# Attention scores from two float32r parts, two heads in the two halves of the array's rows

## The chip, the core and the metric

The kernel runs on one core of a Trainium2 chip. The core has a matrix engine (PE, with its weight loads shown apart as PEld), a vector engine (DVE), a scalar engine (ACT), a general engine (POOL) and SP, which here only issues DMAs. Each engine works through its own instructions in order and waits on semaphores. PE writes to PSUM, eight banks of 128 partitions by 2 KB; DVE and ACT read PSUM, POOL and the DMAs do not. The metric is device time in microseconds. Before the change it was 4454.7 us (median of three runs, 4446.5 to 4455.5).

## The reference

Four attention blocks in a row act on `x` of 16 batches, 512 tokens and 256 channels, all float32, with 16 heads of 16 dims. Each is `x = x + block(layernorm(x))`:

```python
x = x + _L0_attn_a_ref(_layernorm(x), ...)   # causal mask, biases
x = x + _L0_ffn_ref(_layernorm(x), ...)      # tokens in two groups by a similarity, 5 register tokens
x = x + _L0_attn_b_ref(_layernorm(x), ...)   # rotary embedding, no mask
x = x + _L0_ffn_ref(_layernorm(x), ...)
```

Each block projects Q, K and V, takes softmax(Q K^T / 4) over 512 keys, multiplies by V and projects back. In block `f` a token attends only to the tokens of its own group (similarity to a given direction, scaled over the whole batch, above 0.9 or not) and to the registers; the register tokens get the mean of both groups' answers. The similarity of all batches must be known before the first scores of `f`.

## The kernel before, in words

The layers are called 0 (`a`), 1 (`f`), 2 (`b`) and 3 (`f`); `PLAN` lists them. A layer goes through 16 batches, a batch through four *quads* of four heads (`quads`), a quad through four key tiles of 128 (`t`).

**Two sets of scores.** Each head's scores are computed twice. `maxima` (L523) computes them with queries on the partitions, `s` (L545), and DVE takes each row's maximum (L547; in layer 0 with the causal mask added, L552). `finish` and `put` split the maxima into two bf16 numbers, turn them on PE (`mt`, L579), copy them on ACT (`ms`, L581), write them to DRAM (`md`, L583) and from there into two rows of the Q stack (L585). `products` (L594) computes the scores again with keys on the partitions, `t` (L612); those two rows subtract each query's maximum inside the matmul. In layer 0 another matmul adds the causal mask (L620). ACT takes the exponential (`e`, L623), and `weigh` multiplies by V in float32, four heads side by side in four 32-column tiles of the array (`po`, L634).

**Precision.** Q and K are split into three bf16 parts (`split3`, L329) and written to DRAM (`qd`, `kd`). `load_half` (L489) gathers six blocks of 16 rows for eight heads: 96 rows whose product sums the six largest part products. Rows 96 and 97 carry the group flags (from `fd`), 98 and 99 the maxima. There are three such stacks of Q and of K (`NB`), loaded by SP's DMAs.

**Other work** is cut into pieces by generators: `prep` (layer norm, projections, splits, similarity) for the next layer's batch, `tail` (division by the sums, output projection) of the batch before, `registers`, `masked`. `drain` deals pieces out between the scores by the costs that they yield. They use PSUM through `small` (pool `ps_s`, two banks); the scores use `ps_x`, five banks.

**Order.** The last loop (L919) issues four products per key tile, and `advance` runs `maxima` ahead by `AHEAD` = 36 heads' tiles; a quad's `put` follows `WAIT` = 8 steps after its last maximum. A list scheduler then fixes the order of instructions on each engine when the kernel is built. Before the first `f` scores all similarities must be in (`split`), so work does not run ahead across that point.

Of the kernel before, what the change touches and what calls it, by code (L numbers as in the profile page):

```python
# [39 lines left out]
H, D = 16, 16  # L41
# [6 lines left out]
RW = 4 * (32 + REG)  # L48
# [6 lines left out]
AHEAD = 36  # L55
WAIT = 8
QPARTS = (0, 1, 2, 0, 1, 0)
KPARTS = (0, 0, 0, 1, 1, 2)
ROWS = 96
# [3 lines left out]
def constants():  # L63
# [7 lines left out]
    c["mask_t"] = np.ascontiguousarray(f(-BIG) * up.T)  # L71
# [4 lines left out]
    c["cos"], c["sin"] = np.repeat(cos, H, axis=0), np.repeat(sin, H, axis=0)  # L76
    c["hm"] = np.concatenate([np.tile(np.eye(H, dtype=f), (8, 1)), np.zeros((P, H), f)], axis=1)
    blk, half = np.zeros((P, H, HV), f), np.zeros((P, REG), f)
    rows = np.zeros((2, 2, RW), f)
    for h in range(H):  # L80
        p, k = 32 * (h // 4), h % 4
        for r in range(REG):
            blk[p + REG * k + r, h] = 1.0
            half[p + REG * k + r, r] = 0.5
            rows[1, :, (32 + REG) * k + r] = 1.0
    c["blk"], c["half"], c["rows"] = blk, half, rows
    clamp = np.full((P, NT, 4), -MASKED, f)
    clamp[P - 1, NT - 1] = 3.0e38
    c["clamp"] = clamp
    reg = np.zeros((P, B, NT), f)  # L90
# [7 lines left out]
def hybrid_kernel(ctx: ExitStack, tc: tile.TileContext, a: dict, out: bass.AP):  # L98
# [3 lines left out]
    def pool(name, bufs, **kw):  # L102
# [10 lines left out]
        pool("pe", 9),  # L113
# [5 lines left out]
    ps_x = pool("ps_x", 5, space=PSUM)  # L119
    ps_o = pool("ps_o", 1, space=PSUM)  # L120
    ps_s = pool("ps_s", 2, space=PSUM)
# [17 lines left out]
    qd = [dram.tile([3, C, S], BF, tag=f"qd{b}", name=f"qd{b}") for b in range(B)]  # L139
    kd = [dram.tile([3, C, S], BF, tag=f"kd{b}", name=f"kd{b}") for b in range(B)]  # L140
    vd = [dram.tile([P, NT, VW], F32, tag=f"vd{b}", name=f"vd{b}") for b in range(B)]
    xd = [dram.tile([P, NT, C], F32, tag=f"xd{b}", name=f"xd{b}") for b in range(B)]
    fd = dram.tile([4, B, S], BF, tag="fd", name="fd")
    md = [dram.tile([NT, 2, 4, P], BF, tag=f"md{i}", name=f"md{i}") for i in range(8)]
# [10 lines left out]
    ident_bf = const.tile([P, P], BF, tag="ident_bf", name="ident_bf")  # L155
    nc.vector.tensor_copy(ident_bf, ident)
# [5 lines left out]
    def load_weights(layer, project):  # L162
# [7 lines left out]
        for i in ws:  # L170
            raw = ptmp.tile([P, 2, C], F32, tag="tmp", name=f"wraw{layer}_{i}")
            nc.sync.dma_start(raw, a[f"{kind}_w"][:, :, i, :])
            if i == WQ:
                nc.vector.tensor_scalar(raw, raw, SCALE, None, ALU.mult)
            k = 0 if project else i
            nc.scalar.copy(wh[:, :, k, :], raw)
            nc.vector.tensor_tensor(wl[:, :, k, :], raw, wh[:, :, k, :], ALU.subtract)
# [9 lines left out]
    bqk = load_const("bqk", [P, 2, 2])  # L187
# [6 lines left out]
    NB = 3  # L194
    Qs, Ks = [], []
    for i in range(NB):
        q = res.tile([P, 8, S], BF, tag=f"qs{i}", name=f"qs{i}")
        k = res.tile([P, 8, S], BF, tag=f"ks{i}", name=f"ks{i}")
# [8 lines left out]
    for i in range(2):  # L207
        t = res.tile([ROWS + 2, 2, RW], BF, tag=f"rst{i}", name=f"rst{i}")
# [3 lines left out]
    def constant_rows():  # L212
        both = ptmp.tile([4, 2, S], BF, tag="tmp", name="zo")
        nc.vector.memset(both[:, 0], 0.0)
        nc.vector.memset(both[:, 1], 1.0)
        for q, k in zip(Qs, Ks):
            for i, t in enumerate((q, k)):
                nc.sync.dma_start(t[ROWS : ROWS + 4], both[:, i].unsqueeze(1).to_broadcast([4, 8, S]))
        for t in rst:
            nc.gpsimd.memset(t, 0.0)  # L220
# [4 lines left out]
    def early_constants():  # L225
        late["mask_s"] = to_bf("mask_s", [P, S])
        late["mask_t"] = to_bf("mask_t", [P, P])
        late["clamp"] = load_const("clamp", [P, NT, 4])
# [4 lines left out]
    def direction():  # L233
# [13 lines left out]
        )  # L247
        ps = small("gt")
        for i in range(2):
            nc.tensor.transpose(ps[:, i * P : (i + 1) * P], g2[:, i * P : (i + 1) * P], ident)  # L250
# [5 lines left out]
    def late_constants():  # L256
# [7 lines left out]
        rows = p1.tile([2, 2, RW], F32, tag="rows", name="rows")  # L264
        nc.sync.dma_start(rows, a["rows"])
        rb = p1.tile([2, 2, RW], BF, tag="rb", name="rb")
        nc.vector.tensor_copy(rb, rows)
        for t in rst:
            nc.sync.dma_start(t[ROWS : ROWS + 2], rb)
# [5 lines left out]
    def prep(layer, b, x):  # L275
# [53 lines left out]
        def split3(which, i, y):  # L329

            t = p4.tile([P, 3, S], BF, tag="parts", name=f"t{which}{n}_{i}")
            nc.scalar.copy(t[:, 0, :], y)  # L332
            sub = nc.vector if which == "k" and layer + b == 0 else nc.gpsimd
            sub.tensor_tensor(y, y, t[:, 0, :], ALU.subtract)  # L334
            nc.vector.tensor_copy(t[:, 1, :], y)  # L335
            sub.tensor_tensor(t[:, 2, :], y, t[:, 1, :], ALU.subtract)  # L336
            d = (qd if which == "q" else kd)[b]
            nc.sync.dma_start(d[:, i * P : (i + 1) * P, :].rearrange("k p q -> p k q"), t)

        def parts(which, i):  # L340
            ps = small(f"p{which}{n}_{i}")
            yield from project(ps, WQ if which == "q" else WK, i)
            y = ptmp.tile([P, S], F32, tag="tmp", name=f"y{which}{n}_{i}")
            if kind == "a":
                w = 0 if which == "q" else 1
                nc.scalar.activation(y, ps, AF.Identity, bias=bqs[:, w, i : i + 1])
            else:
                nc.scalar.copy(y, ps)
            if kind == "f" and which == "q":
                y2 = ptmp.tile([P, S], F32, tag="tmp", name=f"y2{n}_{i}")  # L350
                nc.scalar.activation(y2, ps, AF.Square)
                st["y", i] = y, y2
            else:
                split3(which, i, y)

        def similar():
# [6 lines left out]
            for i in range(2):  # L363
                split3("q", i, st["y", i][0])
# [14 lines left out]
            else:  # L379
                nc.gpsimd.tensor_tensor(nd[:, 0], nd[:, 0], nhalf, ALU.pow)  # L380
# [4 lines left out]
        def turned(which):  # L385
# [10 lines left out]
            nc.vector.tensor_tensor(b_, y[1], sin, ALU.mult)  # L396
            nc.gpsimd.tensor_tensor(a_, a_, b_, ALU.subtract)
            nc.vector.tensor_tensor(b_, y[0], sin, ALU.mult)
            nc.gpsimd.tensor_tensor(y[1], y[1], cos, ALU.mult)
            nc.gpsimd.tensor_tensor(y[1], y[1], b_, ALU.add)  # L400
            split3(which, 0, a_)
            split3(which, 1, y[1])
# [47 lines left out]
    def split(layer):  # L450
# [22 lines left out]
        fl = p1.tile([P, 4, n], BF, tag="fl", name=f"fl{layer}")  # L473
# [4 lines left out]
        pf = small(f"pf{layer}", BF)  # L478
        for k in range(4):
            nc.tensor.transpose(pf[:n, k * P : (k + 1) * P], fl[:, k, :], ident_bf)  # L480
        fs = p1.tile([n, 4, P], BF, tag="fs", name=f"fs{layer}")
        nc.vector.tensor_copy(fs.rearrange("r k p -> r (k p)"), pf[:n, : 4 * P])
        nc.sync.dma_start(fd.rearrange("k b (t p) -> (b t) k p", p=P), fs)


    halves = [(layer, b, u) for layer in range(len(PLAN)) for b in range(B) for u in range(2)]
    cleared = set()

    def load_half(i):  # L489
        layer, b, u = halves[i]  # L490
        kind = PLAN[layer]
        q, k = Qs[i % NB], Ks[i % NB]
        hs = slice(8 * u, 8 * (u + 1))
        if kind == "b" and i % NB not in cleared:
            cleared.add(i % NB)
            nc.gpsimd.memset(q[ROWS : ROWS + 2].bitcast(F32), 0.0)
        for dst, src, blocks in ((q, qd[b], QPARTS), (k, kd[b], KPARTS)):
            src = src.rearrange("k (d h) s -> (k d) h s", h=H)
            r = 0
            while r < 6:  # L500
                e = r + 1
                while e < 6 and blocks[e] == blocks[e - 1] + 1:
                    e += 1
                p0 = D * blocks[r]
                nc.sync.dma_start(dst[D * r : D * e], src[p0 : p0 + D * (e - r), hs, :])
                r = e
        if kind == "f":
            f = slice(ROWS, ROWS + 2)
            nc.sync.dma_start(q[f], fd[0:2, b, :].unsqueeze(1).to_broadcast([2, 8, S]))
            nc.sync.dma_start(k[f], fd[2:4, b, :].unsqueeze(1).to_broadcast([2, 8, S]))  # L510
# [12 lines left out]
    def maxima(i):  # L523
# [490 lines left out]
```

## Time and profile before

| | |
|---|---|
| profiled execution | 4459.0 us, its span 4457.3 us |
| runs | 4446.5, 4454.7, 4455.5 us |
| granted PE clock, mean | 0.972 |
| busy: PE, DVE, ACT, POOL | 4232, 3392, 2791, 1483 us |
| layers 0, 1, 2, 3, from where their first scores stand | about 60, 1280, 2320, 3480 us |
| PE busy per 200 us in layers 0, 1, 2, 3 | 181 to 190, 199, 198, 193 to 195 |
| DVE busy per 200 us there | 132 to 147, 169 to 176, 153, 160 |
| DMA share in the same layers | 0.45 to 0.51, 0.44, 0.42, 0.40 |
| DMA traffic | 470.6 MB, 42.6% of 16 engines' span |

A group line names the source line, engine, operation, tiles written and read with their shapes, the number of instructions, their busy time and the mean ns of one, then the engine's idle time just before them and what ended most of it. Tile names: `s` and `t` are scores, `e` their exponentials, `po` the weighted sums, `md` the maxima in DRAM, `p..`, `x..`, `ot`, `pa`, `pj`, `r.` the work in between.

### The profile page before, as it was taken

Reading aid. Unit: us, or ns where it says so; the run is one execution under the profiler, and the core shown is the slowest. Engines: PE = TensorE matmul, PEld = TensorE weight load, DVE = VectorE, ACT = ScalarE, POOL = GpSimd, SP = SyncE. Lnnn points to the kernel's source line nnn. Section 1 sums busy time; section 2 is a strip of 40 time slices with the busy share of each in tenths; the row PEclk is TensorE's granted clock in tenths of the full one; section 3 lists DMA queues with packets and bytes.
Section 4 is the critical chain, followed back from the end, with each engine's and each line's share of the span. In section 5 each row is a group of like instructions: output and inputs, shape, how many; then the busy total and the mean of one; then the engine's idle time right before and its main releaser. Section 6 shows DMA issues by size and latency. Waiting matters only on the chain.

```text
span 4457.3 us, 76135 instructions
## 1 busy us (share of the span) xinstructions
PE 4231.9 (95%) x26672; PEld 1995.5 (45%) x26672; DVE 3392.3 (76%) x8003; ACT 2791.5 (63%) x5480; POOL 1482.9 (33%) x1302
## 2 busy tenths in 40 slices
PE   6999899999979999999999999999999799999999
PEld 4555555555534444444444444444444233333333
DVE  6776666777668888888888777777775687887885
ACT  3555455555536767767767666666666466666666
POOL 4445455554432433433433333423424100000000
PEclk8999999999979999999999999999999799999999
DMA  6544545454424444444444443444444144333441
GB/s 176 128 128 122 134 119 141 123 144 116 119 71 101 105 110 108 104 114 103 108 115 107 106 110 101 102 107 103 104 105 113 44 89 89 83 78 83 89 89 30
DMA packets 230020, 470.56 MB, mean 106 GB/s; under 512 B 45630, under 2 KB 176004, under 8 KB 205060
## 3 DMA queue, kind: packets, MB, share of 16 engines
q1 hardware_dynamic: 229636, 465.69, 42.6%
q8 instruction: 211, 3.46, 0.3%
q14 instruction: 173, 1.42, 0.1%
HBM read 291.18 MB, written 174.19 MB: 104 GB/s over the span
## 4 chain that ended last, share of the span: by engine, by line
PE 75%; DMA 12%; DVE 4%; ACT 3%; POOL 2%; issue 2%; SPq 1%; ACTq 0%; POOLq 0%; DVEq 0%
PE po L634 19%; PE t L612 17%; PE s L545 16%; DMA md<-ms 5%; PE pj L833 4%; PE pq L324 3%; PE pv L415 3%; PE pk L324 3%; ACT e L623 3%; DMA x<-in_x 2%; PE ot L793 2%; DMA qs<-qd 2%; PE rs L675 1%; DMA qs<-md 1%; DVE mx L547 1%
## 5 line engine op out<-in xcount | busy, mean ns | idle before, releaser
L623 ACT ACTIVATE e<-t 128x512 f32<-128x512 f32 (+1 forms) x3776 | 2053.4, 594 | 865.7 <-PE t L612 588.7
L547 DVE TENSOR_REDUCE mx<-s 128x1 f32<-128x512 f32 x3072 | 1970.6, 682 | 517.0 <-PE s L545 507.2
L612 PE MATMUL t<-qs,ks 100*128 100x512 bf16 (+3 forms) x4096 | 1422.6, 364 | 61.1 <-DMA qs<-md 37.5
L545 PE MATMUL s<-ks,qs 98*128 98x512 bf16 (+4 forms) x4096 | 1404.9, 367 | 57.9 <-DMA ks<-fd 16.9
L634 PE MATMUL po<-e,v 128*32 128x512 f32 (+1 forms) x8192 | 1071.1, 569 | 7.5 <-ACT e L623 4.9
L612 PEld LDWEIGHTS <-ks 100*128 100x128 bf16 x4096 | 397.8, 98 | 779.1 <-issue 528.9
L545 PEld LDWEIGHTS <-qs 96*128 96x128 bf16 (+1 forms) x4096 | 386.0, 99 | 597.9 <-issue 383.3
L552 DVE CUSTOM_DVE_ANT_0 sc<-s,mask_s_bf 128x128 bf16<-128x128 f32 (+3 forms) x1024 | 497.7, 486 | 172.5 <-PE s L545 134.6
L634 PEld LDWEIGHTS po<-e,v 128*32 128x32 f32 x8192 | 172.2, 108 | 407.6 <-issue 290.2
L380 POOL TENSOR_TENSOR nd<-nd,nhalf 128x64 f32<-128x64 f32 x30 | 316.8, 10561 | 0.0
L290 POOL TENSOR_SCALAR st<-mv 128x4 f32<-128x4 f32 x64 | 16.0, 251 | 884.3 <-DVE mv L287 849.7
L664 POOL COPY rst<-qs 96x40 bf16<-96x40 bf16 x64 | 14.6, 229 | 859.6 <-DMA qs<-qd 336.4
L334 POOL TENSOR_TENSOR yq<-yq,tq 128x512 f32<-128x512 f32 x112 | 131.1, 1177 | 296.9 <-ACT e L623 155.7
L650 ACT COPY o<-po 128x512 f32<-128x512 f32 x256 | 150.8, 589 | 110.5 <-PE po L634 107.8
L789 POOL TENSOR_TENSOR x<-x,f_bo 128x1024 f32<-128x1024 f32 x32 | 76.0, 2376 | 404.2 <-DMA x<-xd 308.1
L620 PE MATMUL t<-mask_t_bf,ident_bf 128*128 128x128 bf16 x1024 | 203.8, 223 | 0.0
L793 PE MATMUL ot<-ident,o 128*128 128x128 f32 x1024 | 182.7, 291 | 18.1 <-DVE vst L427 12.4
L306 POOL TENSOR_SCALAR xn<-x,nm,st 128x256 f32<-128x256 f32 x256 | 142.4, 561 | 116.0 <-PE xp L310 102.7
L332 ACT CAST tk<-yk 128x512 bf16<-128x512 f32 x112 | 69.3, 619 | 173.1 <-DMA qd<-tq 170.3
L793 PEld LDWEIGHTS ot<-ident,o 128*128 128x128 f32 x1024 | 129.4, 148 | 78.0 <-DVE vst L427 15.2
L336 POOL TENSOR_TENSOR tk<-yk,tk 128x512 bf16<-128x512 f32 x110 | 128.3, 1168 | 95.5 <-DVE tk L335 89.8
L335 DVE CAST tq<-yq 128x512 bf16<-128x512 f32 x112 | 88.6, 793 | 77.3 <-POOL yq L334 76.8
(365 smaller groups left out, 5509.4 us busy)
## 6 DMA issues: line engine op xcount, KB each, us to landing
ks<-kd SPq DMA_DIRECT2D x256, 256.0 KB
qd<-tq SPq DMA_DIRECT2D x128, 384.0 KB
qs<-qd SPq DMA_DIRECT2D x128, 384.0 KB
kd<-tk SPq DMA_DIRECT2D x128, 384.0 KB
vd<-vst SPq DMA_DIRECT2D x64, 576.0 KB
v<-vd SPq DMA_DIRECT2D x64, 576.0 KB
qs<-qd SPq DMA_DIRECT2D x128, 256.0 KB
ks<-kd SPq DMA_DIRECT2D x256, 128.0 KB
```

Of the source, the lines that this page charges most:

```text
L324: nc.tensor.matmul(dst, ww[:, c, w, cols], xx[:, c, :], start=(k == 0 and c == 0), stop=(k == 2 and c == 1))
L380: nc.gpsimd.tensor_tensor(nd[:, 0], nd[:, 0], nhalf, ALU.pow)
L545: nc.tensor.matmul(ps, q[rows, h, t * P : (t + 1) * P], k[rows, h, :end], start=True, stop=True)
L547: nc.vector.tensor_reduce(st["mx"][:, t, j : j + 1], ps, AX.X, ALU.max, negate=True)
L552: nc.vector.tensor_tensor_reduce(w, ps, late["mask_s"][:, S - end :], 1.0, -3.0e38, ALU.add, ALU.max, st["mx"][:, t, j - m + 1 + i : j - m ...
L612: nc.tensor.matmul(ps, k[: ROWS + 4, h, t * P : (t + 1) * P], q[: ROWS + 4, h, q0:], start=True, stop=(kind != "a"),)
L620: nc.tensor.matmul(ps[:, :P], ident_bf, late["mask_t"], start=False, stop=True)
L623: st["exp", t] = nc.scalar.activation(e[:, : m * w], st["ps"][:, : m * w], AF.Exp)
L634: mm = nc.tensor.matmul(st["po"][32 * j : 32 * j + 32, q0:], v[:, t, h * HV : h * HV + 32], E.pop((t, j)), start=(t == 0), stop=(t == NT - 1),
L650: nc.scalar.copy(o, st["po"])
L793: nc.tensor.transpose(ps[:, g * P : (g + 1) * P], O[layer, b, g][:, t * P : (t + 1) * P], ident)
L833: nc.tensor.matmul(ps[:, k * C : (k + 1) * C], aa[:, k, c, :], ww[:, c, 0, :], start=(q == 0 and c == 0), stop=(q == 2 and c == 1),)
```

## The change

Q and K are split into two float32r parts, and a head's stack has 48 rows (three blocks of 16) and four more for maxima and flags. Two heads of a pair take partitions 0 to 63 and 64 to 127. Each pair's two matmuls write two neighbouring PSUM banks, and one reduction and one exponential serve both. The stacks, with their constant rows and flags, stand in DRAM as the array reads them; a quad of Q or K comes by one GpSimd DMA. The maxima of eight heads go back together. `ps_x` has three tiles of two banks, `ps_s` one bank. Some rotary products move from DVE to POOL; the long power on POOL is cut into four.

```diff
-AHEAD = 36
-WAIT = 8
-ROWS = 96
+AHEAD = 24
+WAIT = 3
+ROWS = 48
+HALF = 64
...
-        pool("pe", 9),
+        pool("pe", 5),
-    ps_x = pool("ps_x", 5, space=PSUM)
+    ps_x = pool("ps_x", 3, space=PSUM)
-    ps_s = pool("ps_s", 2, space=PSUM)
+    ps_s = pool("ps_s", 1, space=PSUM)
...
-    qd = [dram.tile([3, C, S], BF, tag=f"qd{b}", name=f"qd{b}") for b in range(B)]
+    qd = [dram.tile([2, HALF, H // 2, S], F32, tag=f"qd{b}", name=f"qd{b}") for b in range(B)]
...
-    NB = 3
+    NB = 6
-        q = res.tile([P, 8, S], BF, tag=f"qs{i}", name=f"qs{i}")
+        q = res.tile([P, 2, S], FR, tag=f"qs{i}", name=f"qs{i}")
...
+    def constant_rows(b):
+        for w, d in ((0, qd[b]), (1, kd[b])):
+            for e in range(2):
+                nc.sync.dma_start(d[e, ROWS:], a["zo"][w].unsqueeze(1).to_broadcast([HALF - ROWS, H // 2, S]))
...
+        def send(which, i, t):
+            d = (qd if which == "q" else kd)[b]
+            two, one = (0, 2 * D) if which == "q" else (D, 0)
+            for e in range(2):
+                r = slice(HALF * e, HALF * (e + 1))
+                nc.sync.dma_start(
+                    d[e, two : two + 2 * D].rearrange("(k i d) h s -> i (d h) k s", k=2, i=2)[i],
+                    t[r].bitcast(F32),
+                )
+                nc.sync.dma_start(
+                    d[e, one + 8 * i : one + 8 * i + 8].rearrange("d h s -> (d h) s"), t[r, 0, :].bitcast(F32)
+                )
+
+        def split2(which, i, y):
+            t = p4.tile([P, 2, S], FR, tag="parts", name=f"t{which}{n}_{i}")
+            nc.gpsimd.tensor_copy(t[:, 0, :], y)
+            nc.gpsimd.tensor_tensor(t[:, 1, :], y, t[:, 0, :], ALU.subtract)
+            send(which, i, t)
...
+                nc.scalar.copy(t[:, 0, :], ps)
+                nc.vector.tensor_tensor(t[:, 1, :], ps, t[:, 0, :], ALU.subtract)
+            send(which, i, t)
...
-            nc.vector.tensor_tensor(b_, y[1], sin, ALU.mult)
+            nc.gpsimd.tensor_tensor(b_, y[1], sin, ALU.mult)
...
+        for b in range(B):
+            for k, d in ((0, qd[b]), (2, kd[b])):
+                for e in range(2):
+                    nc.sync.dma_start(
+                        d[e, ROWS + 2 : ROWS + 4].rearrange("k h s -> h k s"),
+                        fd[k : k + 2, b, :].unsqueeze(0).to_broadcast([H // 2, 2, S]),
+                    )
+
+    def load_quad(i):
+        layer, b, g = quads[i]
+        for t, d in ((Qs[i % NB], qd[b]), (Ks[i % NB], kd[b])):
+            nc.gpsimd.dma_start(t, d[:, :, 2 * g : 2 * g + 2, :].rearrange("e r h s -> (e r) h s"))
...
+            if p % m == 0:
+                st["ps"] = ps_x.tile([P, 2, S], F32, tag="x", name=f"s{n}_{g}_{t}_{p}")
+            for e in range(2):
+                r = slice(HALF * e, HALF * e + n_rows)
+                nc.tensor.matmul(
+                    st["ps"][:, e, (p % m) * end :][:, :end],
+                    q[r, p, t * P : (t + 1) * P],
+                    k[r, p, :end],
+                    start=True,
+                    stop=True,
+                )
+            if kind != "a":
+                nc.vector.tensor_reduce(st["mx"][:, :, 2 * g + p, t], st["ps"], AX.X, ALU.max, negate=True)
...
+            def put():
+                ps = small(f"mt{n}")
+                rows = NT * 8
+                nc.tensor.transpose(ps[:rows, :P], mx.rearrange("p j t -> p (j t)"), ident)
+                ms = p2.tile([rows, 2, P], FR, tag="ms", name=f"ms{n}")
+                nc.scalar.copy(ms[:, 0, :], ps[:rows, :P])
+                nc.vector.tensor_tensor(ms[:, 1, :], ps[:rows, :P], ms[:, 0, :], ALU.subtract)
+                d = md[half % len(md)]
+                nc.sync.dma_start(d.rearrange("k e j t p -> (e j t) k p"), ms.bitcast(F32))
+                for g in range(2):
+                    for e in range(2):
+                        r = HALF * e + ROWS
+                        nc.gpsimd.dma_start(
+                            Qs[(2 * half + g) % NB][r : r + 2],
+                            d[:, e, 2 * g : 2 * g + 2].rearrange("k j t p -> k j (t p)"),
+                        )
...
+            if kind == "a":
+                for o in range(2):
+                    for e in range(2):
+                        mk = late["mask_t"][HALF * e : HALF * (e + 1), o]
+                        nc.tensor.matmul(ps[e][:, :P], mk[:, 0], mk[:, 1], start=False, stop=(o == 1))
+            if p % m == m - 1:
+                e_ = pe.tile([P, 2, S], F32, tag="e", name=f"e{n}_{t}_{p}")
+                st["exp", t] = nc.scalar.activation(e_[:, :, : m * w], st["ps"][:, :, : m * w], AF.Exp)
...
-        load_through(min(end // 2 - 1, i // 2 + (2 if i else 1)))
+        load_through(min(end - 1, i + (4 if i else 3)))
...
-            for j in range(4):
-                score(t, j)
-                to = 4 * (NT * i + t) + j + 1 + AHEAD
+            for p in range(2):
+                score(t, p)
+                to = 2 * (NT * i + t) + p + 1 + AHEAD
```

## The prediction

> **What bounds the kernel now.** I read the page first: shares, slices, chain, dearest groups.
>
> ```profile
> span 4457.3 us, 76135 instructions
> PE 4231.9 (95%) x26672; PEld 1995.5 (45%) x26672; DVE 3392.3 (76%) x8003; ACT 2791.5 (63%) x5480; POOL 1482.9 (33%) x1302
> ...
> PE   6999899999979999999999999999999799999999
> ...
> PE 75%; DMA 12%; DVE 4%; ACT 3%; POOL 2%; issue 2%; SPq 1%; ACTq 0%; POOLq 0%; DVEq 0%
> PE po L634 19%; PE t L612 17%; PE s L545 16%; DMA md<-ms 5%; PE pj L833 4%; PE pq L324 3%; PE pv L415 3%; PE pk L324 3%; ACT e L623 3%; DMA x<-in_x 2%; PE ot L793 2%; DMA qs<-qd 2%; PE rs L675 1%; DMA qs<-md 1%; DVE mx L547 1%
> ...
> L623 ACT ACTIVATE e<-t 128x512 f32<-128x512 f32 (+1 forms) x3776 | 2053.4, 594 | 865.7 <-PE t L612 588.7
> L547 DVE TENSOR_REDUCE mx<-s 128x1 f32<-128x512 f32 x3072 | 1970.6, 682 | 517.0 <-PE s L545 507.2
> L612 PE MATMUL t<-qs,ks 100*128 100x512 bf16 (+3 forms) x4096 | 1422.6, 364 | 61.1 <-DMA qs<-md 37.5
> L545 PE MATMUL s<-ks,qs 98*128 98x512 bf16 (+4 forms) x4096 | 1404.9, 367 | 57.9 <-DMA ks<-fd 16.9
> ```
>
> PE is busy in nearly every slice and holds 75% of the chain; ACT and DVE wait for PE, hardly the reverse. But matmul records overlap, so a matmul's price is the distance between starts. That is in PE's timeline, around 2006 us (layer 1) and in a projection:
>
> ```profile
> 2005.70 0.38 PE L545 MATMUL s<-ks,qs 98*128 98x512 bf16 x1
> 2006.02 1.06 PE L634 MATMUL po<-e,v 128*32 128x512 f32 x8
> 2007.01 0.39 PE L612 MATMUL t<-qs,ks 100*128 100x512 bf16 x1
> 2007.24 0.38 PE L545 MATMUL s<-ks,qs 98*128 98x512 bf16 x1
> ...
> 2007.90 0.60 PE L695 MATMUL rt__26323<-ident,re 128*128 128x128 f32 x4
> 2008.33 0.38 PE L612 MATMUL t<-qs,ks 100*128 100x512 bf16 x1
> ```
>
> ```profile
> 1990.51 0.62 PE L324 MATMUL pq<-xh,whq 128*128 128x512 f32 x2
> 1990.97 0.62 PE L324 MATMUL pq<-xh,wlq 128*128 128x512 f32 x2
> ```
>
> A bf16 score costs 0.22 us, a float32r matmul of 512 columns 0.46/2 = 0.23, a load of 128 four-byte columns with a short matmul 0.43/4 = 0.108. Going from a full tile to `po`'s 32-column tiles costs 0.32 - 0.22 = 0.10 extra; leaving them about as much. The eight `po` matmuls take 0.99 together, so four narrow tiles do run side by side. Counts times such distances give a PE stream of 3973 us for the kernel before; the other 484 us of the span are waits and edges.
>
> **The change, part by part.**
>
> *Scores in pairs.* In the layers without a causal mask there are 3072 pairs. Two bf16 matmuls cost 2 x 220 = 440 ns. A pair in two halves of the array's rows appears nowhere in the trace. Lower bound: its two weight loads, 2 x 108 = 216; upper: no overlap, 2 x 227 = 454. I take 227, one float32r matmul, because `po` shows tiles overlapping in columns: -213 x 3072 = **-654 us**. The Trainium skill ("TensorE: Matmul & The Clock Gate", Part 3: Packing small matmuls) reports 3.07 times for four row tiles, 0.77 of ideal. By that a pair would cost 440/1.54 = 286 ns and the gain would be 473 us. The row has the same array and lengths, so I keep 227 and put 181 us into the range.
>
> In the causal layer tiles are short and a pair still needs two four-byte loads (216 ns), where short bf16 matmuls were 0.06 to 0.17 apart; each head gets two mask matmuls for one. If the masks overlap in pairs this saves 62 us, if loads limit it saves 6: **-34**.
>
> *Changes of tile shape.* Row halves are a third shape. Walking the built PE order I count 4076 changes for 2956: 1120 x 0.10 = **+112**. PE's stream alone: **-576 us**.
>
> *One small PSUM buffer instead of two.* Pairs need two banks, so `ps_x` takes six of the eight banks and `ps_s` one. Projections, transposes, register scores and now the turned maxima (1344 groups) follow each other through one bank. A group frees it after its last matmul's tail (0.38 - 0.22 = 0.16), an ACT copy (0.59) and for split results a DVE subtraction (0.69): 0.85 or 1.5 us. PE executes in order, so a next group too near holds the scores behind it, then exp and reduce. Between each group's last and the next group's first matmul I summed the distances in the built order. The shortfalls are 115 us for projections of Q and K, 68 for `xp`, 65 for `ot`, 43 for `pv`, 109 for the rest: 400, against 43 with two buffers before: **+357**. Below nothing is excluded; none is the lower bound, if PE would have waited for score buffers anyway.
>
> *The maxima's way back.* Row maxima go PE transpose `mt` - ACT - SP DMA to `md` - second DMA into the Q stack, before the first product of that half. What the way takes now is in SP's waits (total, times, longest) and the chain near 3930 us:
>
> ```profile
> SPq L583 <- ACT ms L581: 775.6, 179, 18.6
> SPq L585 <- DMA md<-ms: 719.2, 252, 8.3
> ```
>
> ```profile
> 3928.67 6.05 DMA md<-ms
> 3934.74 2.10 DMA qs<-md
> ```
>
> The write lands 719.2/252 = 2.85 us after SP is ready, sometimes 6. Before, the built order puts 8.9 to 15.0 us of PE work (means by layer and group) between `mt` and the product that needs it, so this mostly hides: `t` waited on it 87 us in all. After, `mt` goes through the one small bank, in line with the other groups, and stands late: 3.0 and 1.8 us for the two halves in layer 0, 2.9 and 7.5 in layer 1, 4.4 and 2.1 in layer 2, 7.6 and 6.2 in layer 3. The chain becomes ACT 0.24 + DVE 0.29 (a 32-row operation like L569, 0.30) + SP issue 0.32 + 2.85 + two GpSimd DMAs (the first product needs one for each row half) + landing 2.1. No GpSimd DMA is in the trace. SP's issue of the same transfer takes 0.62; the skill ("DMA: Bandwidth & Descriptors", Anatomy of one DMA) gives about 2.0 us fixed for one, landing included, near 0.62 + 2.1. I take 1.0 to issue each: 7.8, say 8 us. Lower: 6.3 (0.62 issues, 2.1 for the write); upper: 10.2 (6.05 for the write). Counting small-buffer waits inside the window only once, 128 halves fall short by 183 us in all at 6, 364 at 8, 615 at 10: **+364**. Late next are the exps of that quad, then `po`; POOL stands behind the four copies, and behind POOL the normalised inputs of `xp`.
>
> *Hidden otherwise.* DVE: 1536 double reduces at 682 + 533 (512 more elements at 1.04 ns, the slope between L552's 128- and 512-wide rows) save 229 us; L335's casts, `mb` and two rotary products leave, subtractions from PSUM come. ACT: a double exp at about 1028 for 2 x 601, casts leave. Both lie beside PE; only in layer 3 does DVE (43 us a batch) come level with PE's stream (43). POOL: L334 and L336 leave (602 us); 128 copies and subtractions (about 250), 64 rotary products at 1.28, 192 small copies at 0.23 come: 1483 -> about 1260 us. To that 512 stack loads and 512 maxima copies: 640 us at 0.62 each, 2050 at 2.0. Cover is PE's 4400; in layer 1, 30 us of arithmetic and 16 DMAs stand against about 65 us a batch. If that cover is gone, POOL sets the batch. SP: 2106 -> 1650 issues; loads leave, 1024 stores replace 256, so `md` can queue behind stores. Before each layer f there are 64 flag copies; four stand ahead of the first load, 2 x 4 x 0.62 = 5 us. Bytes: loads 201 -> 268 MB, stores 101 -> 201, constants 17: 471 -> about 650 MB, share 43% -> about 58%; in layer 0 about 0.49 -> 0.78. I price that through the chain's upper end.
>
> Sum on the profiled execution: 4457.3 - 576 + 357 + 364 = 4602. That execution took 4459.0; the median is 4454.7. Forecast **4600 us**.
>
> **Rivals.**
>
> *The new waits fall into old ones* (faster). 484 us of the span already were waits or edges; while PE waits for the small bank, exp and reduce empty score buffers that PE would have waited for later. For it: ACT's idle time before exps is 866 us, and layer 0 has gaps already. Against: layers 1 and 2 have PE busy above 97%. It decides once 145 of the 721 us overlap. If half of the 484 absorbs waits: 4602 - 242 = 4360; if all, 4118.
>
> *Row halves don't run side by side.* The pair costs 454, the 654 us become a loss of 43: 4602 + 697 = 5299. Against: `po`'s tiles and the cited measurement.
>
> *POOL or DMA becomes the bound.* Issues of 2.0 us and a loaded DMA system make the way back 10 to 12 us: 615 to 870 for 364, so 4850 to 5110, more if POOL holds `xp` up. For it: layer 0's chain already runs over 10 us input loads. Against: no GpSimd DMA here has a time.
>
> **How the numbers follow.** My case has 0.50, waits falling into waits 0.30, POOL or DMA 0.12, no overlap 0.08. My case reaches 4470 to 4850, the faster 4110 to 4440. The range 4150 to 5100 leaves out the best end of the faster case and most of the no-overlap case, about 2 in 10. Less than 0.2% (9 us) can't be told from no change here; 0.04 falls there, from the edge between the first two. Faster 0.30, slower 0.66.
>
> **What would show it.** Right: `s` and `t` start in twos a few ns apart, pairs about 0.23 apart; PE's busy share falls to about 75 to 80%; the first `t` of each even quad waits for the copy from `md`, longest in layers 0 and 2; projections wait for ACT or DVE readers of the small bank; layer 3 gains, layer 0 loses. Wrong: seconds of pairs start 0.2 us after firsts; or `t` waits for `md` below 150 us in all; or POOL's queue is in the chain.

## The result and the profile after

| | before | after | forecast |
|---|---|---|---|
| median of four runs, us | 4455.1 | 5149.5 (5144.7 to 5166.4) | 4600, range 4150 to 5100 |
| ratio to before, 95% interval | | 1.157 (1.154 to 1.160) | 1.033 |
| profiled span, us | 4457.3 | 5142.9 | 4600 |
| of it PE idle, us | 225 | 857 | |
| of it PE at half clock, us | 252 | 1240 | |

The direction was the likelier one of the forecast (slower, 0.66). The size was not: 694 us were lost where 145 were forecast, and the time lies outside the range.

The page of the changed kernel, the lines that answer to those shown of before:

```profile
span 5142.9 us, 73729 instructions
PE 4285.8 (83%) x27312; PEld 2116.4 (41%) x27312; DVE 3135.9 (61%) x5760; ACT 2480.8 (48%) x3240; POOL 1812.4 (35%) x2421
...
PE   4878878888887688889888988888888769889998
...
PE 45%; ACT 10%; DVE 6%; DMA 5%; issue 3%; POOL 1%; SPq 1%; ACTq 0%; DVEq 0%; POOLq 0%
...
L653 ACT ACTIVATE e<-t 128x1024 f32<-128x1024 f32 (+2 forms) x1920 | 1854.4, 996 | 1141.7 <-PE t L639 767.1
L574 DVE TENSOR_REDUCE mx<-s 128x2 f32<-128x1024 f32 x1536 | 1856.2, 1220 | 691.4 <-PE s L566 663.9
L566 PE MATMUL s<-ks,qs 52*128 52x512 f32 (+4 forms) x4096 | 978.1, 463 | 215.2 <-ACT e L653 115.9
L639 PE MATMUL t<-qs,ks 52*128 52x512 f32 (+4 forms) x4096 | 1038.6, 474 | 142.5 <-DMA qs<-md 114.4
```

PE's busy share fell from 95% to 83%, and its share of the chain from 75% to 45%. DVE went down from 76% to 61%, ACT from 63% to 48%; POOL rose from 33% to 35% and has 1% of the chain. So no engine took over as the bound. PE now loses time at many small hand-overs: its idle time (span less busy time) grew by 632 us, where the forecast put 721 us of waits. Its busy time, which a gain of 576 us should have shortened, rose from 4232 to 4286.

Where the time went is read from PE's timeline. The span is cut at the first `t` of each layer, and each interval from one matmul's start to the next one's is put down to the first of the two: scores (`s`, `t` and the masks), `po`, or other work (projections, transposes and the like). A wait is thus counted behind the matmul that it follows.

| us | layer 0 | layer 1 | layer 2 | layer 3 | behind scores | behind `po` | behind other work |
|---|---|---|---|---|---|---|---|
| before | 1225 | 1050 | 1148 | 947 | 1956 | 1001 | 1412 |
| after | 1633 | 1167 | 1266 | 966 | 1762 | 1083 | 2186 |
| difference | +408 | +117 | +118 | +19 | -194 | +82 | +774 |

The last three differences make 662 us, and the work ahead of the first `t` took 23 more: 685 us, the difference of the spans. The forecast's gain (-576 in scores and changes of shape) is not there: -194 + 82 = -112. The 774 behind other work are not waits alone: steps from other work into a pair are counted there, and so is slower work at half clock.

**The clock.** The trace records PE's clock as granted in full or by half, here in 40 slices of the span, first before the change, then after it:

```profile
PEclk8999999999979999999999999999999799999999
PEclk6889898887987699999999899989899879989999
```

At half clock the same work takes almost twice as long. Two projection matmuls of 512 columns took 0.46 us before (the lines near 1990 us in the prediction). In layer 2 of the changed kernel, in a stretch whose clock is 0.50 (third number from the right in the last line), two take 0.85:

```profile
3455.92 1.05 PE L347 MATMUL pq<-xl,whq 128*128 128x512 f32 x2
3456.77 1.05 PE L347 MATMUL pq<-xh,whq 128*128 128x512 f32 x2
...
3454.00:3458.00 4.00, 4.00 (x13) 2.31 (x13) 1.23 (x1) 2.07 (x3) 1.27 (x1) 0.50 0.63 135
```

After the change 3713 matmuls start at half clock, before it 693. The sum of what each took beyond an undisturbed step of the same kind at full clock (at most as much again) is an estimate of what this costs: 340 us, against 75 before. So PE's own work got about 270 us longer; where it only covered a wait, the span did not grow by it. The drops follow idle time: in the 3.4 us ahead of the 93 drops PE was busy for 0.43 of the time (median), ahead of the rises for 1.00. No run holds the clock and keeps the waits, so what the clock costs by itself is read from the trace only.

**The steps of a run.**

PE's timeline of the changed kernel in layer 2 shows what a step costs (start, duration, instruction):

```profile
3500.44 1.07 PE L665 MATMUL po<-e,v 128*32 128x512 f32 x8
3501.43 0.50 PE L639 MATMUL t<-qs,ks 50*128 50x512 f32 x2
3501.77 0.40 PE L566 MATMUL s<-ks,qs 48*128 48x512 f32 x2
3502.01 0.40 PE L639 MATMUL t<-qs,ks 50*128 50x512 f32 x2
3502.34 0.66 PE L828 MATMUL ot<-ident,o 128*128 128x128 f32 x4
3503.14 0.49 PE L566 MATMUL s<-ks,qs 48*128 48x512 f32 x2
3503.56 1.06 PE L665 MATMUL po<-e,v 128*32 128x512 f32 x8
```

The two of a pair do run side by side. But of a run (pairs with no other work between them) the first pair takes 0.34 us to the next one, only the second 0.24, and the last of a run takes 0.33 to 0.42, where a bf16 matmul before took 0.22. A run of pairs is rarely long: in the layers without a mask `po` or other work comes after one to three pairs in 1251 of 1374 runs.

The same view in layer 0 shows the single small bank. In brackets stands PE's idle time and whom it waited for:

```profile
907.61 0.40 PE L453 MATMUL pv<-whq,xh 128*128 128x256 f32 x2
907.94 0.43 PE L665 MATMUL po<-e,v 128*32 128x128 f32 x8
908.79 0.50 PE L453 MATMUL pv<-whq,xl 128*128 128x256 f32 x2 [0.43 <-DVE vst L465]
...
910.08 0.40 PE L453 MATMUL pv<-whq,xh 128*128 128x256 f32 x2
911.26 0.66 PE L828 MATMUL ot<-ident,o 128*128 128x128 f32 x4 [0.78 <-DVE vst L465]
912.45 0.28 PE L602 MATMUL mt<-ident,mx 128*32 128x128 f32 x1 [0.53 <-DVE xt L832]
913.39 0.65 PE L828 MATMUL ot<-ident,o 128*128 128x128 f32 x4 [0.66 <-DVE ms L605]
914.59 0.44 PE L848 MATMUL pa<-ident,on 128*128 128x128 f32 x2 [0.54 <-DVE xt L832]
```

Each group waits until the one before it has been read. From the last `pv` matmul to an `ot` behind it the median is 1.06 us (0.12 before the change), from the last `pk` to a `pv` 1.84 (0.23 before), where one follows the other directly (13 and 18 cases). The maxima's transpose `mt` stands in the middle of this line.

### The profile page after: what moved, and what is told of

It reads as the page before. It is cut to its first block, busy times and chain, and to the rows that moved or that the text cites. A ratio compares the mean times of both kernels' runs of the same rounds, so it can differ in the third digit from the quotient of the medians.

```text
span 5142.9 us, 73729 instructions
## 1 busy us (share of the span) xinstructions
PE 4285.8 (83%) x27312; PEld 2116.4 (41%) x27312; DVE 3135.9 (61%) x5760; ACT 2480.8 (48%) x3240; POOL 1812.4 (35%) x2421
## 3 DMA queue, kind: packets, MB, share of 16 engines
q1 hardware_dynamic: 202032, 384.02, 24.2%
## 4 chain that ended last, share of the span: by engine, by line
PE 45%; ACT 10%; DVE 6%; DMA 5%; issue 3%; POOL 1%; SPq 1%; ACTq 0%; DVEq 0%; POOLq 0%
PE po L665 14%; PE t L639 8%; PE s L566 8%; ACT e L653 7%; DMA qs<-md 3%; DVE mx L574 2%; PE pv L453 2%; PE pk L347 2%; PE pq L347 2%; DMA md<-ms 2%; PE pj L868 2%; PE ot L828 2%; PE rs L710 1%; PE xp L333 1%; ACT o L681 1%
## 5 line engine op out<-in xcount | busy, mean ns | idle before, releaser
L653 ACT ACTIVATE e<-t 128x1024 f32<-128x1024 f32 (+2 forms) x1920 | 1854.4, 996 | 1141.7 <-PE t L639 767.1
L574 DVE TENSOR_REDUCE mx<-s 128x2 f32<-128x1024 f32 x1536 | 1856.2, 1220 | 691.4 <-PE s L566 663.9
L566 PE MATMUL s<-ks,qs 52*128 52x512 f32 (+4 forms) x4096 | 978.1, 463 | 215.2 <-ACT e L653 115.9
L639 PE MATMUL t<-qs,ks 52*128 52x512 f32 (+4 forms) x4096 | 1038.6, 474 | 142.5 <-DMA qs<-md 114.4
L639 PEld LDWEIGHTS t<-qs,ks 50*128 50x128 f32 (+1 forms) x4096 | 454.2, 202 | 925.3 <-issue 405.7
L534 POOL DMA_DIRECT2D qs<-qd x256 | 145.4, 568 | 1618.4 <-PE s L566 935.9
L566 PEld LDWEIGHTS s<-ks,qs 48*128 48x128 f32 (+1 forms) x4096 | 430.7, 204 | 507.8 <-ACT e L653 291.0
L611 POOL DMA_DIRECT2D qs<-md x512 | 265.8, 526 | 593.3 <-DMA md<-ms 554.8
L418 POOL TENSOR_TENSOR nd<-nd,nhalf 128x16 f32<-128x16 f32 x120 | 345.9, 2900 | 91.3 <-DVE nd L409 91.3
L650 PE MATMUL t<-mask_t_bf 64*128 64x128 bf16 x2048 | 180.4, 247 | 0.0
```

What stands on the lines that cost most here:

```text
L418: nc.gpsimd.tensor_tensor(nd[:, 0, t], nd[:, 0, t], nhalf[:, t], ALU.pow)
L566: nc.tensor.matmul(st["ps"][:, e, (p % m) * end :][:, :end], q[r, p, t * P : (t + 1) * P], k[r, p, :end], start=True, stop=True,)
L574: nc.vector.tensor_reduce(st["mx"][:, :, 2 * g + p, t], st["ps"], AX.X, ALU.max, negate=True)
L611: nc.gpsimd.dma_start(Qs[(2 * half + g) % NB][r : r + 2], d[:, e, 2 * g : 2 * g + 2].rearrange("k j t p -> k j (t p)"),)
L639: nc.tensor.matmul(ps[e], k[rows[e], p, t * P : (t + 1) * P], q[rows[e], p, q0:], start=True, stop=(kind != "a"),)
L650: nc.tensor.matmul(ps[e][:, :P], mk[:, 0], mk[:, 1], start=False, stop=(o == 1))
```

## The experiments

Fifteen kernels were run, e9 once and the others four times. Times are medians, ratios are against the kernel before. The columns behind them are of the profiled execution: those of the table above, and the time at half clock (252 us before, 1240 in the changed kernel).

| run | us | ratio, 95% interval | layers 0, 1, 2, 3 | scores | `po` | other | half clock |
|---|---|---|---|---|---|---|---|
| e1 full tiles | 5411 | 1.216 (1.214 to 1.218) | 1643, 1244, 1380, 1036 | 2368 | 1032 | 1903 | 713 |
| e2 two score tiles, three small banks | 5047 | 1.135 (1.131 to 1.138) | 1371, 1222, 1280, 1088 | 2241 | 1135 | 1585 | 881 |
| e3 single banks | 4968 | 1.117 (1.115 to 1.119) | 1522, 1163, 1215, 956 | 2099 | 1070 | 1686 | 720 |
| e4 no copies of maxima | 5030 | 1.131 (1.129 to 1.132) | 1509, 1322, 1240, 862 | 1845 | 1052 | 2037 | 1011 |
| e5 two score tiles, one small bank | 5443 | 1.226 (1.221 to 1.231) | 1639, 1245, 1363, 1072 | 2186 | 1144 | 1989 | 987 |
| e6 before, one small bank | 4935 | 1.112 (1.110 to 1.114) | 1467, 1114, 1166, 1089 | 2084 | 1026 | 1725 | 607 |
| e7 `mt` through a score tile | 4852 | 1.092 (1.090 to 1.095) | 1481, 1176, 1186, 883 | 1742 | 1059 | 1925 | 901 |
| e8 stacks by SP | 5067 | 1.141 (1.137 to 1.145) | 1619, 1151, 1263, 906 | 1651 | 1061 | 2226 | 1068 |
| e10 e3 and e7 | 4830 | 1.085 (1.081 to 1.090) | 1377, 1128, 1214, 978 | 2112 | 1038 | 1549 | 555 |
| e11 e7, small work in score tiles | 4820 | 1.085 (1.083 to 1.086) | 1444, 1199, 1174, 884 | 1827 | 1033 | 1841 | 898 |
| e12 e11 by SP | 4807 | 1.081 (1.079 to 1.084) | 1416, 1184, 1203, 887 | 1790 | 1010 | 1891 | 868 |
| e13 e7, no copies of maxima | 4821 | 1.082 (1.080 to 1.084) | 1469, 1192, 1162, 887 | 1713 | 1040 | 1959 | 786 |
| e14 e7, full tiles | 5209 | 1.169 (1.167 to 1.172) | 1541, 1286, 1261, 984 | 2365 | 1020 | 1685 | 580 |
| e15 before, small work in score banks | 4557 | 1.023 (1.021 to 1.024) | 1338, 1050, 1147, 936 | 1946 | 1018 | 1505 | 355 |

### What the row halves are worth

**e1.** Both matmuls of a pair over all 128 rows, for `s` and `t` (and the masks) alike:

```diff
-                    q[r, p, t * P : (t + 1) * P],
-                    k[r, p, :end],
+                    q[:, p, t * P : (t + 1) * P],
+                    k[:, p, :end],
```

> Every score matmul contracts over all 128 rows, so the two of a pair are full tiles and follow each other (each then adds up the scores of both heads, and Q is scaled by 0.001 to keep exponentials finite: the values are not the reference's, the counts and shapes of all other work are). By the terms of the prediction (a pair 227 ns, a change of shape 0.10) this loses 0.227 x 3072 = 697 us plus about 100 in layer 0 and wins back about 170 of changes: near 5780 us. By what the trace after shows (a run of pairs costs about 0.10 to enter and 0.19 to leave, and there are 1795 runs in the built order) it wins back 1795 x 0.29 = 520: near 5430, and down to 5230 if the longer stream covers waits for score buffers. Above 5600 the first holds, below it the second.

It took 5411 us, 262 more than the changed kernel: near the second value, far from the first. Behind scores it has 2368 - 1762 = 606 us more, but 283 us of that come back behind other work and 51 behind `po`. Only 141 us of this are idle time of PE (857 to 716). The rest fits what full tiles do not pay: steps from other work into a pair, and work at half clock (1240 to 713 us).

**e9.** The disputed cost by itself: a bench ahead of the work, `halves()` being one pair.

```diff
+        for n in (1, 2, 4, 8):
+            for k in range(12):
+                for m in range(n):
+                    halves()
+                full()
```

> The changed kernel with a bench ahead of its work: runs of 1, 2, 4 and 8 pairs in row halves, twelve times each, with one full float32r matmul between runs, then the same with one group of four narrow float32 matmuls between, then four bf16 full matmuls in place of the pairs. No data is waited for. By the prediction a run of n pairs and the full matmul behind it take 0.227 n + 0.227 + 0.20. If a run costs 0.10 to enter and 0.19 to leave: 0.227 n + 0.227 + 0.29 to 0.30. If the pair itself is dear: a slope near 0.33 instead of 0.227.

From PE's timeline of that run (L941 pairs, L944 the full float32r matmul, L951 the narrow group, L947 bf16):

```profile
23.08 0.50 PE L941 MATMUL two<-qs 48*128 48x512 f32 x2
23.51 0.50 PE L944 MATMUL one<-qs 128*128 128x512 f32 x1
23.95 0.50 PE L941 MATMUL two<-qs 48*128 48x512 f32 x2
...
45.49 1.20 PE L941 MATMUL two<-qs 48*128 48x512 f32 x8
46.62 0.51 PE L944 MATMUL one<-qs 128*128 128x512 f32 x1
47.05 1.20 PE L941 MATMUL two<-qs 48*128 48x512 f32 x8
...
193.78 1.04 PE L947 MATMUL one<-vst 128*128 128x512 bf16 x4
194.46 0.58 PE L944 MATMUL one<-qs 128*128 128x512 f32 x1
194.89 1.04 PE L947 MATMUL one<-vst 128*128 128x512 bf16 x4
...
206.88 1.04 PE L947 MATMUL one<-vst 128*128 128x512 bf16 x4
207.84 1.06 PE L951 MATMUL one<-vst 128*32 128x512 f32 x8
208.84 1.04 PE L947 MATMUL one<-vst 128*128 128x512 bf16 x4
```

From run to run, with the full matmul between, one pair takes 0.865 us, two 1.086, four 1.560, eight 2.500. The slope is (2.500 - 0.865)/7 = 0.234 us a pair, as forecast. What is left at none is 0.865 - 0.234 = 0.631, of which the full matmul is 0.23: entering and leaving a run costs 0.40, twice the forecast's 0.20. With the narrow group between, the periods are 1.420, 1.660, 2.124 and 3.040: slope 0.231, 1.19 at none. Four bf16 matmuls pay nothing beside a full matmul (period 1.113 = 4 x 0.22 + 0.23) and 1.965 - 0.88 = 1.085 beside the narrow group, so there a run of pairs pays 0.10 more than bf16. Set side by side: between full matmuls two pairs take 1.086 us and the four bf16 matmuls that they replace 1.113. A run of two gains 0.03 us there, a run of one loses 0.2, and between narrow groups two pairs gain 0.3. The whole bench lengthens that kernel, so its total time (5395 us) says nothing here.

The built order of the changed kernel has 1795 runs of pairs in all four layers (2.2 pairs each in the layers without a mask). They border on full tiles 1540 times and on narrow ones 2050 times: 1540 x 0.20 + 2050 x 0.05 = 411 us. Narrow tiles have 436 borders fewer in all, which gives back 436 x 0.10 = 44. That is 367 us where the forecast put 112.

The bench has a single full matmul between runs. In the kernel mostly several stand there, and its own trace shows a lower price at full clock:

```profile
1993.22 0.61 PE L347 MATMUL pq<-xl,whq 128*128 128x512 f32 x2
1993.67 0.61 PE L347 MATMUL pq<-xh,whq 128*128 128x512 f32 x2
1994.22 0.50 PE L566 MATMUL s<-ks,qs 52*128 52x512 f32 x2
1994.56 0.39 PE L639 MATMUL t<-qs,ks 52*128 52x512 f32 x2
1994.79 0.40 PE L566 MATMUL s<-ks,qs 52*128 52x512 f32 x2
1995.12 1.06 PE L665 MATMUL po<-e,v 128*32 128x512 f32 x8
```

Two `pq` take 0.45 us before two others and 0.55 before a pair: about 0.09 to enter (medians 0.32 for the last `pq` or `pk`, 0.23 before the change). The three pairs take 0.90 up to `po`, 0.20 more than 3 x 0.233. So a visit costs 0.29 here and not 0.40. From `po` into a pair costs nothing more than before (0.523 us, 0.525 before). The trace has 873 entries from full tiles, 675 exits to them and 1125 exits to narrow ones: 873 x 0.09 + 675 x 0.20 + 1125 x 0.10 = 326, less about 20 for narrow borders that are gone. By these prices the changes of shape cost about 305 us. Both sums are estimates, since layer 0's shorter pairs are charged like the long ones.

### The small bank, the score tiles and the maxima

**e2 and e5.** The eight banks shared out in other ways:

```diff
-    ps_x = pool("ps_x", 3, space=PSUM)
+    ps_x = pool("ps_x", 2, space=PSUM)
-    ps_s = pool("ps_s", 1, space=PSUM)
+    ps_s = pool("ps_s", 3, space=PSUM)
```

e5 makes the first edit alone.

> Two score tiles of two banks instead of three, three small banks instead of one. If the single small bank costs the 357 us of the prediction, and the third score tile is worth little, near 4850. If score tiles are what the later layers lack (in the trace after, s waits for exp about 290 us on the loads), layer 0 gains 150 to 250 us while layers 1 to 3 lose 50 to 150 each: 5000 to 5350 in all.

> Two score tiles of two banks and one small bank: with the changed kernel (three and one) and the second run (two and three) it splits what a score tile and what small banks are worth. By the prediction's 357 us for the small bank: 5047 + 357, near 5400, of which layers 1 to 3 take about 100 each. By the traces so far (the second run won its time in layer 0 alone, 1371 against 1633 us) small banks are worth about 250 in layer 0 and little behind it: 5250 to 5350, layer 0 near 1640.

e2 took 5047 us, e5 5443. So at two score tiles three small banks instead of one are worth 396 us. The profiled executions differ by 358: 268 in layer 0 (1639 against 1371), 23, 83 and -16 behind it. And the third score tile is worth 5443 - 5149 = 294 us, nearly all in layers 1 to 3. e5's total was the prediction's value, its place by layers the other theory's: both prices are high. In e2 the loads of `s` show the lack of score tiles (total, times, longest):

```profile
PEld s L566 <- DVE mx L574: 1214.9, 1092, 3.5
```

In the changed kernel, with three tiles, the same view has these:

```profile
PEld s L566 <- ACT e L653: 291.0, 521, 4.6
...
PEld t L639 <- DVE mx L574: 130.5, 160, 5.1
PEld t L639 <- DMA qs<-md: 119.4, 80, 10.9
```

**e6.** The same edit of `ps_s` in the kernel before, 2 to 1.

> The kernel before with one small bank instead of two and nothing else changed. The prediction's way of counting gives 400 - 43 = 357 us: near 4810. If the price is mostly one of layer 0, where the groups stand close together: 4600 to 4700, two thirds of it in layer 0.

4935 us: 493 more than its runs of before (4443). Both guesses were low. Layer 0 has 242 of it, as the second theory wanted; but layer 3 has 142, where that kernel also sends every fourth group of `s` scores through the small bank. Without layer 3, 324 us are the price of sharing.

**e4.** The four copies into the Q stack left out (the loop over `g` and `e` at the end of `put`).

> Left out: the four GpSimd copies that bring a half's maxima into the Q stack (rows stay zero; Q scaled by 0.001 keeps the exponentials finite). Transposes, splits and the write to DRAM stay. By the prediction's term the way back costs 364 us: near 4785. By the waits in the trace after (t for the copy, about 234 us with those on the loads, partly standing where another wait would) 4920 to 5080.

5030 us, 120 less. The sum hides a caution: the scheduler fixed another order, and layer 1 became 155 us longer although work was taken away. It stood at half clock for 375 us there instead of 195.

**e7.** The transpose of the maxima taken out of the small bank's line. The kernel before also sent it through a score bank:

```diff
-                ps = small(f"mt{n}")
+                ps = ps_x.tile([P, 2, S], F32, tag="x", name=f"mt{n}")[:, 0, :]
```

> The transpose of the maxima goes through a score tile instead of the small bank. In the built order it then stands 9.4 us of PE work ahead of the first product of the half in layer 0 instead of 1.3, and 4 to 5 us in the others as before. If the way back is a cost of its own, it returns a good part of what leaving out the copies returned (120 us): 5030 to 5090, nearly all in layer 0. If the wait for the copy only stands where another wait would stand: 5120 to 5180.

4852 us: 298 less by this line alone, far beyond both guesses, in layers 0, 2 and 3 (152, 80 and 83). It shortens the small bank's line and puts `mt` earlier at once.

**e13.** e7 without the copies.

> The seventh run (transpose of the maxima through a score tile, 4852 us) with the four copies into the Q stack left out (rows stay zero; Q scaled by 0.001). If the way back costs nothing once the transpose stands early: 4820 to 4870. If the two DMAs still hold up products: 120 us less, as in the fourth run, near 4730.

4821 us, 31 less than e7. Once `mt` goes through a score tile, the copies are nearly free; the write to `md` stays in both. So the 298 us of e7 belong to `mt` and the line in front of the small bank, which this edit changes together.

**e14.** e7 with full tiles.

> The seventh run with full tiles instead of row halves, as in the first (each score matmul adds up both heads; Q scaled by 0.001). In the trace of the first run the scores' own time was 606 us longer than in the changed kernel, and 283 us of it disappeared in shorter waits behind other work. If waits for the small bank hid the gain, more of the 606 shows here: 4852 + 350 to 500 = 5200 to 5350. If not: 4852 + 262, near 5110.

5209 us: now the row halves are worth 357 us, not 262, of 623 behind scores. That waits for the small bank hid part of their gain fits this; 240 us still come back behind other work (1925 to 1685).

### PSUM as before, other cover, and the queue

**e3 and e10.** Pairs in row halves, but a bank for each head (five) with a reduction and an exponential each, and two small banks; e10 also sends `mt` through such a bank.

```diff
-    ps_x = pool("ps_x", 3, space=PSUM)
+    ps_x = pool("ps_x", 5, space=PSUM)
-    ps_s = pool("ps_s", 1, space=PSUM)
+    ps_s = pool("ps_s", 2, space=PSUM)
...
-                st["ps"] = ps_x.tile([P, 2, S], F32, tag="x", name=f"t{n}_{t}_{p}")
+                st["ps"] = [ps_x.tile([P, S], F32, tag="x", name=f"t{n}_{t}_{p}_{e}") for e in range(2)]
```

> Pairs stay in row halves, but each head's scores get a bank of their own (five) with a reduction and an exponential each, and the small bank becomes two: the PSUM of the kernel before. DVE and ACT get the shorter, dearer-in-sum instructions back (about 230 and 310 us). If the small bank is the main cost: -357, near 4800. If changes of shape and full buffers hold the pairs up: 4950 to 5100, with only layer 0 clearly better (1633 to about 1400 us) and layers 1 to 3 within 40 us of the changed kernel.

> The third and the seventh run together: a bank of its own for each head's scores, two small banks, and the maxima's transpose through a score bank. If the two gains (181 and 297 us) are of different waits: 4670. If both come from the same line in front of the small bank: 4850, no better than the seventh alone.

4968 and 4830 us. e3 fell where its second theory put it, with a smaller part in layer 0. e10 lies at its second value: the two gains share most of one line. With PSUM and `mt` as before, e10 takes back 637 of the 774 us behind other work. But its scores now take 2112 us, more than the bf16 ones of before (1956). A pair needs two of five banks at once, and the loads of `s` wait for the readers of these banks:

```profile
PEld s L566 <- DVE mx L575: 489.7, 654, 1.7
...
PEld s L566 <- ACT e L655: 151.3, 438, 1.2
```

**e11 and e15.** In layer 0, every second group of the small bank (e11, on e7) or every third (e15, on the kernel before) takes a score tile or bank:

```diff
     def small(name, dtype=F32):
+        turn["n"] += 1
+        if turn["layer"] == 0 and turn["n"] % 2:
+            return ps_x.tile([P, 2, S], F32, tag="x", name=name)[:, 0, :]
```

> The seventh run, and in layer 0 every other group of the small bank also takes a score tile. If layer 0 lacks small banks and not score tiles (the second run had 1371 us there with two score tiles), its 1481 us fall to 1300 to 1380 and the whole to 4680 to 4760; layers 1 to 3 stay within 40 us. If score tiles then lack: near 4850.

> The kernel before, in which every third group of the small banks in layer 0 takes one of the five score banks instead. If two small banks are still too few in layer 0 (its 161 us of longer waits stand behind such groups in part): 40 to 90 us faster, 4360 to 4415. If score banks are as scarce there: within 20 us of 4450, or slower.

e11 took 4820 us and won 37 of the 100 to 180 expected in layer 0: what came back behind other work went out behind scores (429 to 511). e15 lost 100 us, all in layer 0. So this other sharing is worse than the one before the change.

**e8 and e12.** Loads of stacks and copies of maxima by SP instead of GpSimd (the stacks kept as float32 and read as float32r); e12 does so on e11.

```diff
-            nc.gpsimd.dma_start(t, d[:, :, 2 * g
+            nc.sync.dma_start(t, d[:, :, 2 * g
```

> The 512 stack loads and 512 copies of maxima are issued by SP instead of GpSimd. If GpSimd's issues and its waits between them hold up the normalised inputs or the maxima: below 5050. If they lie beside PE, as the chain after says (POOL 1%): 5100 to 5200, or longer, as the copies then stand in SP's queue behind the stores: up to 5300.

> The eleventh run with stacks and maxima issued by SP as in the eighth. The eighth gained 82 us. If that adds up: 80 below the eleventh. If it was only a shorter way back of maxima, which now stand early: within 30 us of it.

5067 us, 82 less, between the two values of e8; 60 are in layer 3. e12 took 4807 us, whose interval overlaps with that of e11. That fits an issue by GpSimd that costs something only while the maxima are late. POOL's busy time fell by 549 us (1812 to 1263), which bought hardly anything.

No version of the changed kernel came below the kernel before; the best, e12, stays 8% above it.

## Why the prediction was wrong

**What bounds the kernel:** right. PE's stream sets the time before, and after the change PE loses time at waits while nothing else is full.

**Scores in pairs (-654, -34):** the pair was right, the place wrong. Side by side a pair costs 0.231 to 0.234 us (e9), against 0.227 taken; the seconds start 3 ns behind the firsts. The lower bound of 216 ns for two weight loads was no bound, since the loads of the two halves run side by side too. But that price holds inside a long run only.

**Changes of tile shape (+112): this step failed.** I took 0.10 us for each change from the narrow tiles of `po`, and only for the 1120 additional ones. In truth the 4096 pairs moved from a shape that pays nothing beside full tiles to one that pays at each visit between them: 0.40 us in e9, 0.29 in the kernel's own trace. Over the built order that makes 305 to 367 us. The Trainium skill ("TensorEngine Tiling (Array Packing)", Tiling Modes, Key Properties) says that changing the tiling mode, not just the tile, drains the engine. This rule speaks against the change, and I did not weigh it; the page gives no price, and these two figures, which agree with it, are the price here.

**The clock: a term that was put at nothing, and this failed too.** All of PE's prices were taken at full clock, with no reason given why it should hold. With 632 us more of idle time, PE stood at half clock for 1240 us instead of 252, and a full matmul then takes 0.427 us and not 0.23. That is worth about 270 us by the estimate above, some 140 of it in scores and `po`.

**Score tiles** were not in my sum either. Three tiles of two banks took the place of five of one, and I said only that pairs need two banks. The third tile is worth 294 us (e5), so three are scarce; what a fourth would bring can't be tried with eight banks. PE's idle time before scores that ends with an exponential or a maximum grew from 42 to 169 us.

Together: PE's busy time should have fallen by 576 us and rose by 54, a gap of 630. The changes of shape explain 190 to 255 of it (305 to 367 less 112) and the half clock about 270. The remaining 105 to 170 stay open; a part is that each of some 800 more waits has the tail of the matmul before it counted as busy (about 0.16 us, the prediction's figure).

**One small bank (+357) and the maxima's way back (+364):** near in sum, wrong in split, and the sum is partly luck. Idle time grew by 632 us for 721, but 126 of it are waits for score tiles, which the 721 did not hold. The bank's price is of the size forecast (396 us from e2 and e5, 324 in the first three layers of e6), half clock included. The way back was forecast at 8 us against short cover; moving `mt` out of the small bank's line is worth 298 us (e7) and the copies behind it then 31 (e13). Counted as the 87 us of before were, `t` waited for the copy 234 us (114 on matmuls, 119 on their loads), so the sign against me, less than 150, did not come. Two small slips: with issues of 1.0 us the chain's upper end is 11.0 us and not 10.2, and the cited 1.54 belongs to 454 ns, which gives 295 and not 286.

**Hidden otherwise:** right, but the DMA share was 42% (24.2 and 18.0 on two queues) and not 58. GpSimd's issue took 0.53 to 0.57 us instead of 1.0, its copy landed in 2.0 us (2.1 taken), and POOL's queue holds 1% of the chain or less.

**The rivals.** *Waits fall into waits* did not show as forecast: idle time rose by most of the 721. It did work against the change: without row halves idle time is 141 us shorter (e1). *No overlap* is refuted by the 3 ns and by e9. *POOL or DMA*: moving the issues from GpSimd to SP gains 82 us (e8), and the DMA share did not grow.

**By layers:** layer 0 was to lose and loses most (408 us). It holds 407 of the 988 us more at half clock (530 after 123), and three small banks win 268 us there (e2 against e5). Layer 3 was to gain and loses 19.

## What to carry to other kernels

Price a tile shape by runs, not by matmuls: walk the built order, and charge each run of row halves 0.29 to 0.40 us between full tiles (0.10 more than bf16 between narrow ones). Between full tiles that takes one and a half to two pairs to earn back. Take PE's prices at the clock that the change will leave: a change that adds waits can also slow the work between them, so look at the granted clock before calling the rest a wait. Before a change spends PSUM banks, ask what each bank bought: here the second small bank and moving one small transpose were each worth about 300 us or more, as much as the row halves themselves (262 in e1, 357 in e14). And a shorter stream gives its time back only where PE is what the others wait for.

## What was unexpected of the hardware

- Weight loads of the two row halves overlap: in the changed kernel those of a pair start 3 ns apart and take 0.19 us each, and the pairs of e9 follow each other at 0.231 to 0.234 us.
- A visit of row halves between full tiles costs 0.40 us with one full matmul between visits (e9) and 0.29 behind several (changed kernel); between 32-column tiles it costs 0.10 more than one of full bf16 tiles.
- The granted clock fell from 0.972 to 0.879. The median distance of full float32r matmuls hides what that means (230 ns before, 235 after, for projections of Q and K): the clock is full or half, and at half the distance is 427 ns. The fall stands for 988 us more at half clock.
- A GpSimd DMA of 512 KB is issued in 0.57 us and lands 4.4 to 5.2 us after its issue, one of 8 KB in 0.53 and 2.0.
